# A two-layer graph attention kernel: the residual moves to other buffers, and the list schedule plans with measured transfers

## The chip, the cores and the metric

The kernel runs on one core of a Trainium2 chip. The metric is the device time of one execution in microseconds (us). A run is one execution; where a kernel was run several times the median stands for it.

## The reference, cut to what matters

There are 32 graphs (batches) of 512 nodes with 512 features, each with its own adjacency matrix. Per batch, two graph attention layers follow a layer norm:

```python
h = jnp.maximum(_layernorm(x, axis=-1), 0.0)
x = x + gnn(adj, h, W1, att_src1, att_dst1, b1, W2, att_src2, att_dst2, b2)

def gat_layer(x, mask, W, a_src, a_dst, bias, concat):
    xl = (x @ W).reshape(B, N, H, F)
    asrc = jnp.einsum('bnhf,hf->bnh', xl, a_src)
    adst = jnp.einsum('bnhf,hf->bnh', xl, a_dst)
    e = leaky_relu(asrc[:, :, None, :] + adst[:, None, :, :], 0.2)
    e = jnp.where(mask[..., None], e, -1e9)
    attn = softmax(e, axis=1)
    out = jnp.einsum('bsdh,bshf->bdhf', attn, xl)
    ...
    return out + bias
h = elu(gat_layer(h, mask, W1, ..., concat=True))   # 4 heads of 256
h = gat_layer(h, mask, W2, ..., concat=False)       # 1 head of 512
```

The last line of the computation matters here: the result is the residual x, plus the second layer, plus its bias b2.

## The kernel before, in words

All is float32. Four large products per batch are the work of the tensor engine (PE): the first projection (`project1`, L823), the gathering with the attention weights of layer 1 (`gather1`, L921), the second projection (`project2`, L977), and the gathering of layer 2 (`gather2`, L1055). Apart from the first batch and the last they are done by a scheme of seven half-size products in place of eight (`sevens`, L734): sums of blocks are made beforehand (`sums` L693, `sums1` L874, `sums2` L1029, on the vector engine DVE), and each of the seven partial products is taken from PSUM into its output block by an evacuation: by ACT as a copy where the block is first written, by DVE as an addition or subtraction where it exists.

The attention weights come from class `Soft` (L543): `first` makes the row sums of the softmax (ACT and DVE alternate on tiles named l), `second` makes the weights p (DVE), adds the mask, and takes the exponential (ACT). The mask is added by a transfer that accumulates from DRAM into SBUF (`accumulate`, L324, issued by POOL; rows named `p<-dm`). Vectors are spread over the partitions by a round trip through DRAM (`spread`; rows `das`, `as`, `drr`, `rr`).

The loop over batches is a software pipeline: one turn holds the heads 0 and 1 of layer 1 of batch i+1 (`gather1(s, 0)`), the first projection of batch i+2, the heads 2 and 3 (`gather1(s, 1)`), the gathering of layer 2 of batch i (`gather2`), and the second projection of batch i+1.

Buffers are handed out by `Slots`. Two sets matter here. The four `xr` buffers of 128x512 are the scratch of `elu` (L841: two ACT ops, then one DVE op that writes h1). The four `t` buffers of the same size hold two right-hand sums (t1, t2) for each head of a pair in `sums1`: the first products read them, and the last reader is a subtraction `b21 - t2` (the name `late` in `gather1`), which is queued before the last product of each head.

The residual (`residual`, L1012) takes four `xr` buffers per batch, loads x into them (SP), and lets an accumulating transfer add b2 (POOL). `gather2` adds its products into these tiles (DVE, `put`), and a transfer from there stores the output (SP); then the buffer is free. Batch 30 uses other places for it.

The order of all this is not written by hand. The code only adds jobs to a `Program` (L45) with an engine, a cost in us, what they read and write, and for transfers a size. `order` (L169) makes one order of all 14462 jobs, and each engine's queue follows from it. PE's own order is the order of the code. The others are list schedules: the planner goes backwards from the end (`backwards`), takes each job's latest start as its rank, goes forwards (`forwards`) and, whenever an engine is free, takes the ready job of the best rank (`next_job`). It does so in 12 rounds and keeps the best. A transfer is modelled as one pipe with a lead, a rate and a tail (L53); a wait between two engines costs 0.15 us, and 0.1 us on the same engine (L52).

Of the kernel before, what the change touches and what calls it, by code (L numbers as in the profile page):

```python
# [44 lines left out]
class Program:  # L45
# [5 lines left out]

    CROSS, SAME = 0.15, 0.1  # L52
    DMA_LEAD, DMA_TAIL, DMA_RATE = 1.2, 1.0, 280e3  # L53

# [21 lines left out]
    def latency(self, a, b):  # L76

        if self.jobs[a][0] != self.jobs[b][0]:
            return self.CROSS
        return 0.0 if self.jobs[a][0] == "PE" else self.SAME  # L80

    def forwards(self, rank):

        jobs, after = self.jobs, self.after
        n = len(jobs)
        left = [len(job[2]) for job in jobs]
        ready_at, start, landed = [0.0] * n, [0.0] * n, 0.0
        free, soon, ready = defaultdict(float), defaultdict(list), defaultdict(list)
        tensor = deque(j for j in range(n) if jobs[j][0] == "PE")
        for j in range(n):  # L90
            if not left[j] and jobs[j][0] != "PE":
                heappush(soon[jobs[j][0]], (0.0, j))
        done = []
        while len(done) < n:
            j, t = self.next_job(rank, free, soon, ready, tensor, left, ready_at)
            start[j] = t
            free[jobs[j][0]] = t + jobs[j][1]
            done.append(j)
            if jobs[j][4] is not None:
                landed = max(landed, t + jobs[j][1] + self.DMA_LEAD) + jobs[j][4] / self.DMA_RATE  # L100
            for s in after[j]:
                if jobs[j][4] is not None:
                    r = landed + self.DMA_TAIL
                else:
                    r = t + jobs[j][1] + self.latency(j, s)
                ready_at[s] = max(ready_at[s], r)
                left[s] -= 1
                if not left[s] and jobs[s][0] != "PE":
                    heappush(soon[jobs[s][0]], (ready_at[s], s))
        return start, done  # L110

    def backwards(self, rank):
# [9 lines left out]
        while True:  # L122
            for j in found:
                if jobs[j][4] is not None:
                    moving = max(moving, ready_at[j]) + jobs[j][4] / self.DMA_RATE
                    ready_at[j] = moving + self.DMA_LEAD
                if jobs[j][0] != "PE":
                    heappush(soon[jobs[j][0]], (ready_at[j], j))
# [13 lines left out]

    def next_job(self, rank, free, soon, ready, tensor, left, ready_at):

        best = None
        for e in ("PE", "ACT", "DVE", "POOL", "SP"):
# [4 lines left out]
            elif ready[e]:  # L151
                t = free[e]
            elif soon[e]:
                t = max(free[e], soon[e][0][0])
            else:
                continue
            if best is None or t < best[0]:
                best = (t, e)
# [10 lines left out]
    def order(self):  # L169
# [8 lines left out]
        for j in reversed(range(n)):  # L178
            later = self.DMA_LEAD + self.DMA_TAIL + (jobs[j][4] or 0.0) / self.DMA_RATE
            need[j] = max(  # L180
# [6 lines left out]
            if jobs[j][0] == "PE":  # L187
                if pe is not None:
                    need[j] = max(need[j], need[pe] + jobs[pe][1])
                pe = j  # L190
        rank, best, self.tried = need, None, []
        for _ in range(self.ROUNDS):
            back = self.backwards(rank)
            late = [-back[j] - jobs[j][1] for j in range(n)]
            start, done = self.forwards(late)
            end = max(start[j] + jobs[j][1] for j in range(n))
            self.tried.append(end)
            if best is None or end < best[0]:
                best = end, start, done, late
            rank = [-start[j] - jobs[j][1] for j in range(n)]  # L200
        _, self.start, done, self.late = best
        return done

    def emit(self):
# [5 lines left out]
def tile_gat(  # L210
# [113 lines left out]
    def accumulate(size, reads, writes, to, at, cost=0.95):  # L324
        prog.add(
            "POOL", cost, reads, writes,
            lambda: nc.gpsimd.dma_start(to, at, accum_op=OP.add), 1.4 * size,  # L327
        )
# [25 lines left out]
    def weights1():  # L354
        for c in range(2):
            for r in range(2):
                for k in range(KQ):
                    row = (r * KQ + k) * P
                    ix = AT[r, c]
                    dma(  # L360
                        256e3, (), [("w1", ix, k)], w1_sb[:, ix, k, :, 2:],
                        w1[row : row + P, :].rearrange("p (j c f) -> p c j f", j=H // 2, c=2)[:, c],
                    )

    def scores1():

        vk, bc = ps_.take()
        for a, v in enumerate((as1, ad1)):
            for j in range(H // 2):
                dma(  # L370
                    256e3, (), [vk + ("v", a, j)], bc[:, 2 * a + j, :],
                    bass.AP(tensor=v.tensor, offset=v.offset + j * 2 * FH, ap=[[0, P], [1, 2 * FH]]),
                )
# [20 lines left out]
    def weights2():  # L394

        for (r, c), ix in AT.items():
            dma(
                512e3, [("ht", 0, 0)], [("w2", ix)], w2_sb[:, ix, :, 1 - c : W2H - c],
                w2[r * HF // 2 : (r + 1) * HF // 2, c * DO // 2 : (c + 1) * DO // 2].rearrange(
                    "(k p) f -> p k f", p=P  # L400
                ),
            )
        dma(4e3, (), ["b1"], b1_sb[:, 0], b1.rearrange("(c p) -> p c", p=P))
        dve(TINY, ["b1"], ["b1"], nc.vector.tensor_scalar_mul, b1_sb[:, 1], b1_sb[:, 0], -1.0)
        dma(256e3, (), ["b2"], b2_sb, rows_of(b2, P))
        for a, v in enumerate((as2, ad2)):
            lk, bc = ls.take()
            dma(256e3, (), [lk], bc, rows_of(v[0], P))
            for (r, c), ix in AT.items():
# [24 lines left out]
    def load(b):  # L434
        XT[b] = []
        for t in range(NT):
            xk, xt = xs.take()
            dma(256e3, (), [xk], xt, x[b, t * P : (t + 1) * P, :])
            XT[b].append((xk, xt))

    def masks(b):

        for t in range(NT):
            ak, a = adjs.take()
            dma(256e3, (), [ak], a, adj[b, t * P : (t + 1) * P, :])
            dve(
# [10 lines left out]
        if b < B - 1:  # L457
            MASK[b] = mk, md = mds.take()
            dma(512e3, every, [mk], md.rearrange("p t n -> p (t n)"), m.rearrange("p t n -> p (t n)"))
        tk, mt = mts.take()  # L460
# [4 lines left out]
            ),  # L465
            300e3,
        )
# [22 lines left out]
    def norm_turn(b, t):  # L490
# [3 lines left out]
        act(  # L494
            0.62, [xk, sk + (t,)], [xk], hn, hn, AF.Relu,
            bias=st[:, t, S : S + 1], scale=st[:, t, S + A : S + A + 1],
# [13 lines left out]
        else:  # L510
# [3 lines left out]
            act(  # L514
                1.14, [xk], [ak], words.rearrange("p (h f) -> p h f", h=2),
                hn.bitcast(U16).rearrange("p (f h) -> p h f", h=2), AF.Copy,
# [6 lines left out]
                ),  # L523
                200e3,
            )
            act(
                1.14, [xk], [("ht", t, 0), ("ht", t, 1)],
                ht[:, :, t * P : (t + 1) * P].bitcast(U16).rearrange("p k (n h) -> p h k n", h=2),
# [14 lines left out]
    class Soft:  # L543
# [7 lines left out]
        def spread(self, v, keys, rows, to, through):  # L551
# [11 lines left out]
            dma(  # L563
                0, [ok], [dk], dr[:k].rearrange("k (b j) -> b k j", j=32),
                bass.AP(
# [4 lines left out]
            dma(  # L570
                256e3 * rows, [dk], [ok], o[:, :rows].rearrange("p r n -> p (r n)"),
                bass.AP(tensor=dr.tensor, offset=dr.offset, ap=[[0, P], [1, rows * N]]),
# [67 lines left out]
        def second(self, h):  # L640
# [19 lines left out]
            if not here:  # L660
                mk, md = MASK[self.b]
                for us in (0, 1), (2, 3):
                    keys = p_keys(pk, us)
                    accumulate(
                        500e3, keys + [mk], keys,
                        *(t[:, us[0] : us[-1] + 1].rearrange("p t n -> p (t n)") for t in (p, md)),
# [67 lines left out]
    def sevens(left, right, rkeys, put, kh, units, width, order):  # L734
# [3 lines left out]
        for u, n in order:  # L738
            m = units[u][0]
            acc, first = {1: "a", 2: "g", 5: "b", 6: "a", 7: "a", 3: "b", 4: "a"}[n], n in (1, 2, 5)  # L740
            if first:
# [4 lines left out]
            pe(  # L746
                akeys + rkeys(n), [bk], kh * width / 597,
                [
# [48 lines left out]
    def project1_first(zt):  # L797

        for j in range(H // 2):
            zk, z = zt[j]  # L800
            for t in range(NT):
                for c in range(2):
# [5 lines left out]
                           for q in (("w1", AT[r, c], k), ("w1s", AT[r, c], k, j))],  # L808
                        [bk], KT * 0.435,
                        [  # L810
# [29 lines left out]

    def elu(g, places, at, cost):  # L841

        keys = [("h1", g, r) for r in range(2)]
        ek, e = xrs.take()
        act(cost, [*places, "b1"], [ek], e, at, AF.Exp, bias=b1_sb[:, 0, g : g + 1], scale=-1.0)
        act(0.54, [ek], [ek], e, e, AF.Relu, bias=1.0, scale=-1.0)
# [6 lines left out]
    def gather1_plain(soft, heads):  # L853

        for h in heads:
            pk, p = soft.p.pop(h)
            for f in range(FPH):
                bk, ps = banks.take()
                for s in range(NT):
# [8 lines left out]
                    )  # L868
                elu(h * FPH + f, [bk], ps, 0.6)
                banks.give(bk)  # L870
# [50 lines left out]
    def gather1(soft, j):  # L921
# [4 lines left out]
        for i, n in PAIR:  # L926
# [5 lines left out]
            if first:  # L932
# [4 lines left out]
            pe(  # L937
                akeys + wkeys, [bk], KQ * M / 597,
                [
# [17 lines left out]
            if n in (3, 4):  # L957
                elu(g, [("h1", g, q) for q in range(2)], h1[:, g, :], 0.54)
        for i in range(2):
# [51 lines left out]

    def residual(b, places=(xrs,) * NT):  # L1012

        XR[b] = []
        for d in range(NT):
# [5 lines left out]
            halves = [xk, xk + (0,), xk + (1,)]  # L1021
            dma(256e3, (), halves, xr, x[b, d * P : (d + 1) * P, :])
            if places[0] is xrs:
                accumulate(256e3, [xk], halves, xr, rows_of(b2, P))
            else:
# [29 lines left out]
    def gather2(b, soft, blocks, order=LAST):  # L1055
# [4 lines left out]
        def put(n, u, bk, ps):  # L1060
# [7 lines left out]
            if n == 4 or r == 0 and upper[u[0]] == 0:  # L1068
                upper[u[0]] = -1
                dma(256e3, [xk, xk + (0,), xk + (1,)], (), out[b, d * P : (d + 1) * P, :], xt)  # L1070
                place.give(xk)
# [9 lines left out]
    def gather2_plain(b, soft):  # L1081
# [3 lines left out]
        for d in range(NT):  # L1085
# [8 lines left out]
            dve(0.6, [bk, xk], [xk], nc.vector.tensor_add, xr, ps, xr)  # L1094
            dma(256e3, [xk], (), out[b, d * P : (d + 1) * P, :], xr)
            banks.give(bk)
# [166 lines left out]
```

## Time and profile before

| | us |
|---|---|
| median of 8 runs | 2867.24 |
| lowest and highest | 2855.19, 2873.09 |
| the profiled execution | 2865.74 |
| its span, first to last instruction | 2863.7 |
| busy in the span: DVE | 2584.6 |
| busy in the span: ACT | 2306.0 |
| idle time of ACT ahead of `p<-p,z`, ended by transfers `p<-dm` | 80.0 |
| idle time of ACT ahead of `l<-as,z`, ended by transfers `as<-das` | 97.5 |
| issue to landing of `p<-dm`, median | 5.1 |
| issue to landing of the b2 addition, median | 5.8 |
| mean granted clock of PE, share of full speed | 0.99 |

The engines are PE (matmul), DVE (vector), ACT (scalar), POOL and SP. The work of POOL and SP here is nearly all issuing of transfers. A float32 matmul appears as two records. Nearly every instruction is recorded under the line of a helper (L316 for ACT, L319 for DVE, L322 for SP, L327 for POOL, L333 for PE), so groups are told apart by their tiles: `xr<-mm,xr` is the addition of a product into the residual. A row of the timeline ends with the idle time before it and who ended it. A wait row gives the total in us, the number of times and the longest.

### The profile page before, as it was taken

The page shows a single profiled execution, that of the slowest core. Times are in us where ns is not written, and L with a number is a line of the kernel's source. Part 1 is how long each engine was busy: PE and PEld are TensorE (multiplying, and loading weights), DVE is VectorE, ACT ScalarE, POOL GpSimd, SP SyncE. Part 2 cuts the span into 40 slices and gives each one's busy share as a digit, 9 for nine tenths or more (in the row PEclk, how much of TensorE's full clock was granted, in tenths as well). Part 3 has the DMA queues.
Part 4 walks back from the last instruction along what each step waited for, and adds up shares of the span by engine and source line. Part 5 has one row for each costly group of instructions (what it writes and reads, how often), then busy time and mean ns, then how long its engine had stood idle before and what let it go on. Part 6 is the DMA issues. An engine that isn't in the chain of part 4 may idle for free. (4 is left out here: it accounts for less than half of the span.)

```text
span 2863.7 us, 41534 instructions
## 1 busy us (share of the span) xinstructions
PE 2777.6 (97%) x12456; PEld 2366.0 (83%) x12456; DVE 2584.6 (90%) x6567; ACT 2306.0 (81%) x4861; POOL 418.6 (15%) x466
## 2 busy tenths in 40 slices
PE   7999999999999999999999999999999999999997
PEld 6668887888888888888888888888888888888875
DVE  7969998999989999999899999999998999999995
ACT  6868787888877888887888888888878888888872
POOL 0011111111111111111111111111111111111100
PEclk9999999999999999999999999999999999999999
DMA  6577687777776777877777867778767778778724
GB/s 203 151 162 192 176 215 175 186 196 188 183 196 173 193 196 192 208 187 186 189 186 186 208 174 186 198 192 203 194 173 193 192 184 216 179 185 203 167 67 129
DMA packets 389455, 527.23 MB, mean 184 GB/s; under 512 B 227184, under 2 KB 231280, under 8 KB 389232
## 3 DMA queue, kind: packets, MB, share of 16 engines
q1 hardware_dynamic: 327600, 332.68, 41.5%
q0 software_dynamic: 61632, 191.92, 30.5%
q8 instruction: 99, 1.62, 0.2%
q14 instruction: 124, 1.02, 0.1%
HBM read 344.72 MB, written 50.79 MB: 138 GB/s over the span
## 5 line engine op out<-in xcount | busy, mean ns | idle before, releaser
L333 PE MATMUL mm<-w_sb,hs 128*128 128x257 f32 (+1 forms) x3024 | 694.7, 383 | 20.4 <-ACT xl L316 11.7
L333 PEld LDWEIGHTS mm<-w_sb,hs 128*128 128x128 f32 x3024 | 573.9, 191 | 116.4 <-ACT xl L316 22.7
L327 POOL DMA_DIRECT2D p<-dm x304 | 268.9, 886 | 2038.0 <-DVE p L319 1089.8
L316 ACT ACTIVATE l<-as,z 128x512 f32<-128x512 f32 x640 | 441.8, 724 | 108.7 <-DMA as<-das 97.5
L316 ACT ACTIVATE p<-p,z 128x512 f32<-128x512 f32 x640 | 433.1, 722 | 109.7 <-DMA p<-dm 80.0
L316 ACT ACTIVATE l<-l,low 128x512 f32<-128x512 f32 x640 | 459.3, 723 | 70.7 <-DVE low L319 68.9
L333 PE MATMUL mm<-p,xl 128*128 128x256 f32 (+1 forms) x2016 | 490.2, 391 | 7.3 <-ACT p L316 5.7
L319 DVE SCALAR_TENSOR_TENSOR p<-rr,z 128x512 f32<-128x512 f32 x640 | 456.9, 742 | 40.1 <-DMA rr<-drr 39.6
L333 PE MATMUL mm<-w_sb,ht 128*128 128x258 f32 x2112 | 481.4, 382 | 2.5 <-ACT xl L316 1.5
L333 PE MATMUL mm<-w_sb,h 128*128 128x257 f32 x2056 | 470.0, 380 | 6.0 <-DVE h L319 4.3
L319 DVE CUSTOM_DVE_ANT_1 l<-l,mt 128x512 f32<-128x512 f32 x640 | 426.3, 681 | 43.4 <-ACT l L316 41.8
L333 PEld LDWEIGHTS mm<-w_sb,ht 128*128 128x128 f32 x2112 | 400.5, 190 | 64.3 <-ACT xl L316 3.8
L333 PEld LDWEIGHTS mm<-p,xl 128*128 128x128 f32 x2016 | 382.7, 190 | 84.5 <-issue 18.6
L333 PEld LDWEIGHTS mm<-w_sb,h 128*128 128x128 f32 x2056 | 389.9, 190 | 65.5 <-DVE h L319 5.3
L316 ACT ACTIVATE xl<-mm 128x258 f32<-128x258 f32 (+2 forms) x752 | 282.2, 385 | 55.1 <-PE mm L333 52.6
L319 DVE TENSOR_TENSOR xl<-xl,mm 128x258 f32<-128x258 f32 x558 | 223.7, 416 | 36.4 <-PE mm L333 27.6
L316 ACT ACTIVATE h<-mm 128x256 f32<-128x256 f32 x480 | 175.2, 378 | 78.9 <-PE mm L333 76.7
L316 ACT ACTIVATE xr<-h,b_sb 128x512 f32<-128x512 f32 x240 | 171.4, 723 | 80.9 <-DVE h L319 80.6
L333 PE MATMUL mm<-t,hs 128*128 128x256 f32 x960 | 218.2, 380 | 0.5 <-ACT h L316 0.5
L333 PEld LDWEIGHTS mm<-t,hs 128*128 128x128 f32 x960 | 183.2, 191 | 26.0 <-ACT h L316 0.8
L319 DVE TENSOR_TENSOR xr<-mm,xr 128x256 f32<-128x256 f32 (+1 forms) x424 | 170.1, 415 | 31.3 <-PE mm L333 21.0
L319 DVE SCALAR_TENSOR_TENSOR h<-h,b_sb,xr 128x512 f32<-128x512 f32 x240 | 175.4, 743 | 20.1 <-ACT xr L316 19.5
(105 smaller groups left out, 3423.7 us busy)
## 6 DMA issues: line engine op xcount, KB each, us to landing
p<-dm POOLq DMA_DIRECT2D x304, 512.0 KB, 5.1
rr<-drr SPq DMA_DIRECT2D x160, 512.0 KB
x<-in_x_dram SPq DMA_DIRECT2D x129, 256.0 KB
adj<-in_adj_dram SPq DMA_DIRECT2D x128, 256.0 KB
as<-das SPq DMA_DIRECT2D x64, 512.0 KB
xr<-in_x_dram SPq DMA_DIRECT2D x124, 256.0 KB
xr<-in_L_gnn_b_dram POOLq DMA_DIRECT2D x124, 256.0 KB, 5.8
out_dram<-xr SPq DMA_DIRECT2D x124, 256.0 KB
```

Source lines behind the costliest of these rows:

```text
L316: prog.add("ACT", cost, reads, writes, lambda: nc.scalar.activation(*a, **k))
L319: prog.add("DVE", cost, reads, writes, lambda: f(*a, **k))
L327: lambda: nc.gpsimd.dma_start(to, at, accum_op=OP.add), 1.4 * size,
L333: f(*a, **k)
```

## The change: what it does

Two things. First, the residual takes the four `t` buffers in place of the four `xr` buffers. The loads, the additions of b2, the additions of products and the stores are the same instructions on other tiles. `elu` has the `xr` buffers to itself.

Second, the planner's figures and its search change. Costs of transfers become times in the pipe by kind (0.75 us for 256 KB, 2.2 for a mask addition, 1.56 for a b2 addition, 1.44 for a spread of two rows), lead and tail change, waits between engines differ by pair, and five ACT costs change. SP and POOL are held back while the planned pipe has more than 3.5 us of work ahead of them. After the 12 rounds follow 40 repairs: wherever the planned PE has a gap over 0.05 us, the jobs that lead to it, back to 60 us before, get an earlier rank by twice the gap, and the schedule is made again; the best of all is kept.

```diff
-    CROSS, SAME = 0.15, 0.1
-    DMA_LEAD, DMA_TAIL, DMA_RATE = 1.2, 1.0, 280e3
+    CROSS, SAME = 0.15, 0.07
+    PAIRS = {("PE", "ACT"): 0.21, ("PE", "DVE"): 0.21, ("DVE", "POOL"): 0.58, ("POOL", "DVE"): 0.4}
+    DMA_LEAD, DMA_TAIL, AHEAD = 0.8, 2.0, 3.5
...
-                landed = max(landed, t + jobs[j][1] + self.DMA_LEAD) + jobs[j][4] / self.DMA_RATE
+                landed = max(landed, t + jobs[j][1] + self.DMA_LEAD) + jobs[j][4]
...
+    def sooner(self, rank, start, cause):
+        jobs, lost, free = self.jobs, {}, 0.0
+        for j in range(len(jobs)):
+            if jobs[j][0] != "PE":
+                continue
+            gap, free = start[j] - free, start[j] + jobs[j][1]
+            d = cause[j]
+            while gap > 0.05 and d is not None and start[j] - start[d] < self.SPAN:
+                lost[d] = max(lost.get(d, 0.0), gap)
+                d = cause[d]
+        return [r - self.GAIN * lost.get(j, 0.0) for j, r in enumerate(rank)]
+
+    SPAN, GAIN = 60.0, 2.0
...
+            if e in ("SP", "POOL"):
+                t = max(t, hold)
...
+        for _ in range(self.REPAIRS):
+            rank = self.sooner(rank, start, cause)
+            start, cause = look(rank)
...
+    REPAIRS = 40
...
-            lambda: nc.gpsimd.dma_start(to, at, accum_op=OP.add), 1.4 * size,
+            lambda: nc.gpsimd.dma_start(to, at, accum_op=OP.add), size,
...
-    def residual(b, places=(xrs,) * NT):
+    def residual(b, places=(ts_,) * NT):
...
-            dma(256e3, (), halves, xr, x[b, d * P : (d + 1) * P, :])
-            if places[0] is xrs:
-                accumulate(256e3, [xk], halves, xr, rows_of(b2, P))
+            dma(0.75, (), halves, xr, x[b, d * P : (d + 1) * P, :])
+            if places[0] is ts_:
+                accumulate(1.56, [xk], halves, xr, rows_of(b2, P))
```

## The prediction

> **What bounds the kernel now.** I read the page's first two parts, then who kept the tensor engine waiting, then its timeline and the chain at those waits.
>
> ```profile
> span 2863.7 us, 41534 instructions
> ...
> PE 2777.6 (97%) x12456; PEld 2366.0 (83%) x12456; DVE 2584.6 (90%) x6567; ACT 2306.0 (81%) x4861; POOL 418.6 (15%) x466
> ```
>
> PE is busy 97% of the span. From the timeline a 256-column product takes 1.73 us per eight records (2682.12 to 2683.85), so the 3.24 million columns that the records hold need about 2736 us. That is the floor, and the change touches no product. Only waits and slow clock can be won. The waits of PE are:
>
> ```profile
> PE mm L333 <- DVE hs L319: 19.6, 7, 6.1
> PE mm L333 <- ACT p L316: 14.1, 7, 8.4
> PE mm L333 <- DVE xr L319: 13.9, 18, 2.2
> PE mm L333 <- ACT xl L316: 13.2, 15, 4.4
> PE mm L333 <- ACT x L316: 10.4, 1, 10.4
> PE mm L333 <- DVE h L319: 5.1, 3, 4.3
> ```
>
> With the two rows left out (3.1 and 1.8) it is 81.2 us. By place on the timeline some 30 us lie before 200 us (filling) and 15 us after 2700 us (last batch), where little can be reordered. The rest is spread over the 29 steady batches; its largest pieces are:
>
> ```profile
> 462.57 5.15 PE L333 MATMUL mm<-x,hs 128*128 128x256 f32 x16 [4.14 <-DVE hs L319]
> ...
> 817.82 2.07 PE L333 MATMUL mm<-xl,hs 128*128 128x256 f32 x4 [2.23 <-DVE xr L319]
> ...
> 1687.93 5.16 PE L333 MATMUL mm<-x,hs 128*128 128x256 f32 x16 [3.08 <-DVE hs L319]
> ...
> 2209.52 5.41 PE L333 MATMUL mm<-x,hs 128*128 128x256 f32 x16 [2.72 <-DVE hs L319]
> ```
>
> Each first group should take 3.5 us (16 records) and takes over 5: the clock fell too. The windows around two of them (columns: us, PE, PEld, DVE, ACT, POOL busy, granted clock, DMA share, GB/s):
>
> ```profile
> 810.00:830.00 20.00, 17.23 (x65) 13.96 (x64) 14.73 (x43) 9.53 (x24) 2.59 (x3) 0.83 0.52 127
> ...
> 2205.00:2225.00 20.00, 17.28 (x73) 14.51 (x72) 17.22 (x48) 12.36 (x27) 2.59 (x3) 0.91 0.77 197
> ```
>
> The waits on DVE xr have their reason in the chain (start, length, what):
>
> ```profile
> 2546.34 0.76 DVE h L319
> 2547.12 5.94 DMA xr<-in_x_dram
> 2553.10 0.47 issue
> 2553.58 5.21 DMA xr<-in_L_gnn_b_dram
> 2558.82 0.75 DVE xr L319 x2
> ```
>
> The ELU's last op frees an xr buffer, the residual is loaded into it, b2 is added by a second transfer, and only then can DVE add the product: 12 us in series, started by an op that comes late.
>
> **The change, part by part.** Every engine keeps the same instructions with the same shapes (PE's order is even the same product by product), so no work is removed or added; the planner's further rounds cost nothing on the chip. What moves is order and one set of buffers.
>
> *Residual in the t buffers.* A t buffer is free after the last subtraction that reads t2, which stands before the last two products of each head; an xr buffer only after those products, their evacuations and three ELU ops. In the new queues the fourth b2 add of a batch stands earlier by a median 5.2 us of tensor work (by over 2.5 in 26 of the 31 batches, leaving the first aside), so the 12 us series starts that much sooner. The xr class of waits (13.9 us, longest 2.2) should vanish.
> Moved with it: four loads on SP and four b2 adds on POOL per batch. In the first batch nothing holds them any more, so they go into the filling: four 256 KB loads between batch 1's x loads, and three b2 adds ahead of the small POOL op that finishes batch 1's norm. Cost: at least 0; at most some 4 us, since the third add waits for its load (5.9 us in the chain above) while the norm's own x loads land anyway. The trace spaces its four x loads there by 0.6 us each; two ahead make 1.2 us. I take 1.5.
> The new wait: the first subtraction into a t buffer of the next pair of heads must wait for the store of the residual (116 such pairs of store and op, where the next ELU had waited before, nearly always with 19 us or more of tensor work between). Queued behind it on DVE is everything, evacuations of PSUM included. Between the last add into a buffer and that subtraction the new DVE queue holds 4.7 us of work at the least and 10.4 in the median. The semaphore times of the 124 stores in the trace give 3.6 us from add to landing in the median, under 5.8 in nine of ten, 8.3 at most. [...] By the row about a tenth are late by 1 us or so, some 10 us of DVE, of which PE sees perhaps 3. I take the row, and count it among the new waits below.
>
> *New costs, hold-back and repair rounds.* I weighed them on the queues of the built program. For each product that waited over 0.2 us I added up the step lengths (0.60 us for a 128x512 DVE op, 0.62 and 0.80 on ACT, from the chain) of all that stands on the producer's queue up to the producer, before and after. Measured from the end of the product before, the steady part (200 to 2700 us) has 50 such waits, 45.4 us. For 40 of them, 33.7 us, the producer now stands earlier by more than the wait: every evacuation into the residual (median 2.6 us), and the sums at 1688 and 2209 us by 8.4 and 8.7. Four, 7.4 us, are covered in part, by 4.1; the one at 462 us is of these (2.0 of 4.3, and its exponentials stand 1.0 later, so a transfer may decide it). Six, 4.3 us, are not covered. Recovered: 33.7 + 4.1 = 37.8 us.
> Given back: 22 clusters of products that did not wait have their producer, mostly an ACT evacuation, moved later than its slack, in total 21 us if queue work were time. ACT idles 19% and DVE 10%, so part of it vanishes in idle time: between 0 and 21. But the trace also shows the mask transfers landing after 5.1 us in the median and 6.85 us in the chain at 2594 us, a spread that no order foresees, so I take 15, above the middle.
> *Clock.* [...] after 2.23 us at 817 the window grants 0.83, after 2.72 at 2209 it grants 0.91. [...] by the rows three waits (817, 1688, 2209) bring (0.17 + 0.09 + 0.09) x 20 = 7 us, less what lies in the gaps themselves: 5.5. I take the rows.
> Steady part: -37.8 + 15 - 5.5 = -28.
>
> *Filling and last batch.* Before 200 us three waits are covered (3.4 us), those at 115 and 188 us by 3.2 and 1.2, the sums at 52 us stand 1.5 later, and the residual loads cost 1.5: -5, of which I count -3, as loads decide there. After 2700 us five small waits (2.5) are covered and about as much is moved later; the last 8.4 us wait has no shift: -1.
>
> **Sum.** -28 - 3 - 1 = -32 us on the span: 2832, hence 2834 for the profiled execution (2865.7, which is 2.0 above its span). The median of the runs, 2867.2, is 1.5 above that execution: 2835.
>
> **Rivals.**
> *The given-back waits are as large as the queues allow* (chance 0.15). ACT evacuations are now later in the first product, all 21 us are paid and the clock drops move elsewhere: -37.8 + 21 = -17, nothing at both ends: 2850. For: rows such as ACT xl, 13.2 us, are hardly relieved. Against: the idle shares.
> *It does not carry over* (0.07). The chip's transfers vary as before, and 45 us of waits come back at other places: about 2865. For: the old order had a plan too. Against: the xr class has a structural reason, and that goes.
> *The store holds DVE* (0.05, slower). If stores land later, because loads for the next batch are now queued beside them, each of 29 batches stops DVE at the subtraction. PE has about 1 us of slack there. It turns the sign when the store lands 4.7 + 1 + 1.1 = 6.8 us after its add in every batch (29 x 1.1 = 32); at 7.3 it costs 29 x 1.6 = 46: 2881. Against: nine of ten are under 5.8 today.
> *More comes* (0.08). No new waits at all, 15 us better: 2820.
>
> **How the numbers follow.** Forecast 0.65 (2826 to 2846), rivals 0.15, 0.07, 0.05 and 0.08. A difference under 0.3% (8.6 us) cannot be told from none here, so faster means under 2858.6: the forecast, the better case and most of the first rival, 0.87; same 0.08; slower 0.05. The range takes in the forecast, most of the better case and the first rival with its spread: 2820 to 2857.
>
> **What would show it.** PE's waits fall from 81 to about 50 us; DVE xr nearly disappears from them; DVE hs keeps the 6.1 at the start and part of the 4.1 near 460 us; no clock below 1.00 in the windows near 817, 1688 and 2209; busy times of all engines are as before. POOL's b2 adds come before the last ELU of their batch. Wrong would be: DVE t waiting for stores over 15 us in all, ACT xl waits above 20 us, or a first 200 us longer by over 4 us.

## The result, and the profile after

The changed kernel takes 2848.57 us (median of 11 runs, 2843.21 to 2854.52), the kernel before, run beside it, 2865.98 (32 runs). The ratio is 0.9943, 95% interval 0.9929 to 0.9957: 17 us faster, about half of the 32 forecast. The profiled execution took 2857.45, more than any of those 11 runs, so a second execution of the same program (`same_again` below, 2845.90) is read beside it.

The head of the page, then who kept PE waiting (total us, times, longest), in the first of the two:

```profile
span 2855.7 us, 41575 instructions
...
PE 2770.0 (97%) x12456; PEld 2359.3 (83%) x12456; DVE 2581.6 (90%) x6567; ACT 2310.5 (81%) x4861; POOL 421.1 (15%) x466
```

```profile
PE mm L368 <- ACT p L351: 19.3, 13, 8.6
PE mm L368 <- ACT xl L351: 17.6, 22, 2.5
PE mm L368 <- DVE hs L354: 15.1, 7, 10.5
PE mm L368 <- ACT x L351: 10.2, 2, 9.9
PE mm L368 <- ACT h L351: 7.4, 7, 2.1
PE mm L368 <- DVE t L354: 7.1, 7, 2.9
PE mm L368 <- DVE h L354: 3.0, 4, 1.4
```

With two small rows (1.1 and 0.4) that is 81.2 us, the same sum as before. The residual's row fell from 13.9 (DVE xr) to 7.1 (DVE t, its new buffers) and the sums (DVE hs) from 19.6 to 15.1; ACT's four rows p, xl, x and h rose from 40.8 to 54.5. The span is 8.0 us shorter, and 7.6 of them came from PE's busy time (2777.6 to 2770.0). As no product changed, that is the clock: the time at half clock fell from 55.5 to 41.8 us, worth half of the difference, 6.9 (in the trace before, 16 records of 256 columns took 5.15 us at 462.57, 2.9 of them at half clock, and 3.62 at 1751.91). Five windows of 20 us, of which the second and the fifth were shown before the change (columns as there; the third number from the end is the granted clock):

```profile
420.00:440.00 20.00, 17.50 (x74) 14.70 (x73) 18.13 (x45) 14.75 (x34) 0.30 (x1) 0.91 0.60 156
810.00:830.00 20.00, 20.00 (x94) 17.46 (x93) 19.89 (x48) 13.88 (x31) 3.04 (x4) 1.00 0.65 198
1680.00:1700.00 20.00, 20.00 (x94) 17.44 (x93) 20.00 (x51) 18.21 (x41) 4.45 (x5) 1.00 0.60 176
2157.00:2177.00 20.00, 17.21 (x71) 14.11 (x70) 17.98 (x45) 16.91 (x38) 1.56 (x2) 0.91 0.52 137
2205.00:2225.00 20.00, 19.04 (x87) 16.30 (x88) 20.00 (x56) 17.97 (x42) 4.23 (x5) 1.00 0.48 151
```

The drops near 817, 1688 and 2209 us are gone (0.83 and 0.91 before in the two windows shown then). Two new ones stand near 427 and 2164. They follow new waits, the second and the fourth row here. The first row is the longest wait of all, in the filling; after the third the clock did not fall:

```profile
55.95 0.80 PE L368 MATMUL mm<-w_sb,hs 128*128 128x258 f32 x1 [10.48 <-DVE hs L354]
425.81 0.48 PE L368 MATMUL mm<-w_sb,ht 128*128 128x258 f32 x1 [2.50 <-ACT xl L351]
984.92 0.48 PE L368 MATMUL mm<-x,hs 128*128 128x256 f32 x1 [2.92 <-DVE t L354]
2163.66 0.94 PE L368 MATMUL mm<-w_sb,hs 128*128 128x258 f32 x2 [2.28 <-ACT xl L351]
```

The transfers that POOL issues (KB each, median us from issue to landing) are slower than before, when the masks took 5.1 and the b2 additions 5.8:

```profile
p<-dm POOLq DMA_DIRECT2D x304, 512.0 KB, 5.8
t<-in_L_gnn_b_dram POOLq DMA_DIRECT2D x124, 256.0 KB, 8.5
```

**Old waits and new ones, site by site.** PE does the same products in the same order, so each product can be compared with itself. In the steady part I took the products that waited over 0.2 us for an evacuation or a sum. A wait counts from the end of the product before, which lasts 1.73 us per eight records of 256 columns. The table has the sums in us:

| products | before | after, first execution | after, second |
|---|---|---|---|
| the 40 whose producer now stands early enough | 33.7 | 0.3 | 1.5 |
| the 4 covered in part | 7.3 | 1.8 | 1.8 |
| the 6 not covered | 4.3 | 0.7 | 0.8 |
| products that had not waited | 0 | 46.0 (52 of them) | 35.6 (43) |

So 42.5 and 41.2 us were won, and 46.0 and 35.6 came back elsewhere. 31 of the new sites are the same in both executions (29.4 and 25.8 us there): most of what came back belongs to the order, and about 10 us of it to the execution.

### The profile page after: what moved, and what is told of

It reads as the page before. It is cut to its first block, busy times and chain, and to the rows that moved or that the text cites. A ratio compares the mean times of both kernels' runs of the same rounds, so it can differ in the third digit from the quotient of the medians.

```text
span 2855.7 us, 41575 instructions
## 1 busy us (share of the span) xinstructions
PE 2770.0 (97%) x12456; PEld 2359.3 (83%) x12456; DVE 2581.6 (90%) x6567; ACT 2310.5 (81%) x4861; POOL 421.1 (15%) x466
## 5 line engine op out<-in xcount | busy, mean ns | idle before, releaser
L368 PE MATMUL mm<-w_sb,hs 128*128 128x257 f32 (+1 forms) x3024 | 695.8, 383 | 25.8 <-ACT xl L351 14.6
L368 PEld LDWEIGHTS mm<-w_sb,hs 128*128 128x128 f32 x3024 | 574.4, 191 | 121.9 <-ACT xl L351 25.8
L351 ACT ACTIVATE l<-as,z 128x512 f32<-128x512 f32 x640 | 442.1, 716 | 88.7 <-DMA as<-das 86.1
L368 PE MATMUL mm<-xl,p 128*128 128x256 f32 (+1 forms) x752 | 181.7, 391 | 11.4 <-ACT p L351 10.4
```

What stands on the lines that cost most here:

```text
L351: prog.add("ACT", cost, reads, writes, lambda: nc.scalar.activation(*a, **k))
L368: f(*a, **k)
```

## The experiments

Each ratio is to the kernel before, run on the same chip. A change of the planner or of the buffers gives all queues a new order, so such a run prices that order as a whole; only `b2_narrow` and `store_narrow` keep the order of the changed kernel. First the switches of the change in one table; the runs follow.

| residual in | planner's figures | hold-back | repairs | ratio, 95% interval | run |
|---|---|---|---|---|---|
| xr | old | no | no | 1 | before |
| t | old | no | no | 1.0089 (1.0055 to 1.0124) | res_only |
| xr | old | no | 40 | 1.0018 (1.0006 to 1.0031) | repairs_alone |
| t | old | no | 40 | 0.9907 (0.9883 to 0.9932), again 0.993 (0.991 to 0.995) | old_times, old_times_again |
| xr | measured | yes | 40 | 1.0149 (1.012 to 1.0178) | plan_only |
| t | measured | yes | none | 1.0067 (1.0049 to 1.0084) | no_repair |
| t | measured | no | 40 | 1.0083 (1.006 to 1.0106) | no_hold |
| t | measured | yes | 40 | 0.9943 (0.9929 to 0.9957), again 0.9947 (0.992 to 0.9973) | after, same_again |

**The changed kernel once more (`same_again`).** No edit.

> The changed kernel unchanged, for a second profile beside the others. Its first profiled execution took 2857.5, above all of its 11 runs (median 2848.6), with 81 us of PE waits, as many as before. Theory (order made for mean transfer times; each execution's own transfer times decide which small waits come up): the median is again 2847 to 2851, and the second profile shows PE waits of 70 to 81 us with the small waits in the steady part at partly other places. Rival (the new waits are fixed by the order): the same places wait by the same amounts within 0.3 us.

2852.89 us, ratio 0.9947. Its profiled execution has PE busy for 2767.6 us and waits of 71.9 us, against 2770.0 and 81.2 in the first. Two executions of one program thus differ by some 10 us in PE's waits, and a forecast from one of them can hardly be checked more closely than that.

**The move alone (`res_only`).** The kernel before, its planner untouched, with

```diff
-    def residual(b, places=(xrs,) * NT):
+    def residual(b, places=(ts_,) * NT):
```

> The kernel before with only the residual moved to the t buffers; planner's figures and search as before. Theory (the buffer move alone removes the waits on DVE xr, 14 to 18 us, and gives back few): 2850 to 2855, waits on DVE t under 5 us, the waits on DVE hs at two or more places stay. Rival (without measured times the planner cannot use the freedom): 2862 to 2868, waits on DVE t of 12 us or more.

2890.01 us, slower by 0.9% and outside both expectations. The waits of PE:

```profile
PE mm L333 <- DVE hs L319: 31.4, 24, 3.9
PE mm L333 <- ACT p L316: 28.2, 14, 8.3
PE mm L333 <- ACT xl L316: 13.1, 14, 4.8
```

The waits on the residual did vanish (1.0 us is left), as the prediction had it. But sums and exponentials, 19.6 and 14.1 us before, took more than that back. Freeing a buffer earlier gave the list schedule another order, not a better one.

**The new planner alone (`plan_only`).** The reverse edit on the changed kernel.

> The changed kernel with the residual in the xr buffers as before: new figures, hold-back and repairs alone. Theory (the move is what gains): 2858 to 2866, waits on DVE xr 10 us or more remain. Rival (the schedule gains and the move adds little): 2848 to 2853, waits on DVE xr under 5 us.

2910.78 us, slower by 1.5% and far above both expectations, and the residual is what PE waits for:

```profile
PE mm L368 <- DVE xr L354: 54.7, 44, 4.6
PE mm L368 <- DVE hs L354: 18.5, 16, 3.2
...
p<-dm POOLq DMA_DIRECT2D x304, 512.0 KB, 5.1
xr<-in_L_gnn_b_dram POOLq DMA_DIRECT2D x124, 256.0 KB, 6.0
```

Rows for `xr` went from 13.9 to 54.7 us: in the xr buffers the series of load and b2 addition still begins at the ELU, and the new order leaves it no slack. The masks land as fast as in the kernel before (5.1).

**The changed kernel without repairs (`no_repair`).**

```diff
-    REPAIRS = 40
+    REPAIRS = 0
```

> The changed kernel without the 40 repair rounds (figures, hold-back and move kept). Theory (the repairs close gaps of the plan, which the chip opens elsewhere): within 4 us of the changed kernel, 2845 to 2853. Rival (the repairs carry the gain): 2858 or more.

2886.67 us, slower than before by 0.7%, as the rival had it. Move and measured figures without repairs lose what the whole change wins.

**Narrow b2 additions (`b2_narrow`).** The order of the changed kernel; each addition moves 32 of 512 columns, so the output lacks b2 in the others.

```diff
-                accumulate(1.56, [xk], halves, xr, rows_of(b2, P))
+                accumulate(1.56, [xk], halves, xr[:, :32], rows_of(b2[:32], P))
```

> The changed kernel with every queue in the same order, but each b2 addition of the steady batches moves 32 of 512 columns, so b2 is left out of the other 480. Theory (the waits that took the place of the old ones end in transfers, and the earlier b2 additions lengthen the mask transfers beside them: 5.1 us before, 5.8 after): 6 to 10 us less than the changed kernel beside it (about 2840 to 2846), mask transfers back at 5.1 to 5.3 us, PE waits on ACT p 5 us lower. Rival (the new waits are the order of ACT's and DVE's queues): within 3 us of the changed kernel, 2847 to 2854.

2840.93 us, ratio 0.9894 (0.986 to 0.9928), below the changed kernel's by 0.5%. The interval lies only just below that of the changed kernel's first series (from 0.9929) and overlaps that of its second (from 0.992). The time is where the theory had it, but not by its mechanism, for the masks land no sooner:

```profile
p<-dm POOLq DMA_DIRECT2D x304, 512.0 KB, 5.9
```

So the bytes of b2 may cost something, but they are not why the masks land later. One thing did change: the three longest transposes of the mask (below) land after 11.0 to 12.3 us, where the changed kernel has 17.5 to 19.9. Whether the 0.5% arise there stays open: the profiled execution was the slowest of the four runs.

**Narrow stores (`store_narrow`).** The same order; each store moves 32 of 512 columns, and the rest of the output is not written.

```diff
-   dma(0.75, [xk, xk + (0,), xk + (1,)], (), out[b, d * P : (d + 1) * P, :], xt)
+   dma(0.75, [xk, xk + (0,), xk + (1,)], (), out[b, d * P : (d + 1) * P, :32], xt[:, :32])
```

> The changed kernel with every queue in the same order, but each store out of a t buffer moves 32 of 512 columns, so most of the output of these batches is not written. Theory (a late store stops DVE for some 8 us in all, and PE sees 3): 2844 to 2852. Rival (the wait of the next t buffer for the store is what gives the gain back): 2840 or less, and waits on DVE t and hs fall by 8 us.

2856.79 us, ratio 0.9953 (0.9938 to 0.9967): no gain, as the theory had it. Nor did the edit take the wait away. The first row is the changed kernel, the second this one, whose profiled execution was its slowest run:

```profile
DVE t L354 <- DMA out_dram<-t: 8.3, 3, 4.2
```

```profile
DVE t L354 <- DMA out_dram<-t: 18.8, 6, 5.4
```

The run therefore doesn't price the wait. What does is the first row: three stops of DVE in 116 chances, 8.3 us of an engine that is idle for 274 us of the span.

**Repairs on the old figures (`old_times`, and once more).** The changed kernel, but all planned costs, rates and waits of the kernel before, and no hold-back:

```diff
-    CROSS, SAME = 0.15, 0.07
-    PAIRS = {("PE", "ACT"): 0.21, ("PE", "DVE"): 0.21, ("DVE", "POOL"): 0.58, ("POOL", "DVE"): 0.4}
-    DMA_LEAD, DMA_TAIL, AHEAD = 0.8, 2.0, 3.5
+    CROSS, SAME = 0.15, 0.1
+    PAIRS = {}
+    DMA_LEAD, DMA_TAIL, AHEAD = 1.2, 1.0, 1e9
...
-                accumulate(1.56, [xk], halves, xr, rows_of(b2, P))
+                accumulate(256e3, [xk], halves, xr, rows_of(b2, P))
```

> The move to the t buffers and the 40 repair rounds, but with the figures of the planner before (transfers, waits, ACT costs) and no hold-back. Theory (repairs help only as far as the planned times are those of the chip): 2865 to 2885, with PE waits on masks and spreads. Rival (the repairs alone carry it, whatever the figures): 2843 to 2856.

2847.98 us. My theory at that point was that the repairs gain only because they work on measured times. It fell: without the measured times the kernel shows no loss.

> The same kernel as old_times, once more: residual in the t buffers, 40 repairs, the planner's figures of the kernel before and no hold-back. Theory (the move and the repairs together carry the gain, the measured figures add nothing): 0.990 to 0.995 of the kernel before again. Rival (the first result was a lucky chip): 0.995 to 1.00. The waits of PE should again sum to some 70 to 80 us, at places that differ from those of the first profile where they end in transfers.

2848.81 us. The result holds on another chip. The two intervals overlap with those of the changed kernel, so this version is not shown to be the faster one; it is the smaller change. Measured as in the table of sites, its steady waits are 48.8 and 47.6 us in the two profiles, no fewer than before (45.3). It wins in the filling: the product that began at 204.2 us before begins at 191.9 and 192.4.

**More repairs (`more_repairs`).** `REPAIRS = 160`.

> The changed kernel with 160 repair rounds in place of 40. Theory (what is left of waits comes from transfers that land later than planned, which a better plan does not see): within 5 us of the changed kernel, 2845 to 2855. Rival (the search was cut short): 2842 or less, and steady waits of PE lower by 8 us.

2858.29 us, ratio 0.995 (0.9931 to 0.9969). Four times the search changes nothing that can be measured.

**Repairs alone (`repairs_alone`).** The kernel before with the repairs, everything else old.

> The kernel before with the 40 repairs alone: its own figures, and the residual left in the xr buffers. Theory (move and repairs need each other, as the residual's chain of load and b2 addition starts at the ELU however the queues stand): the waits on DVE xr stay, 14 us or more in all, and the time is 0.997 to 1.003 of the kernel before. Rival (the repairs do it alone, and the move only came with them): 0.990 to 0.995, waits on DVE xr under 5 us.

2875.24 us. The first four wait rows:

```profile
PE mm L368 <- ACT xl L351: 25.3, 35, 2.2
PE mm L368 <- ACT p L351: 11.9, 7, 3.8
PE mm L368 <- DVE hs L354: 11.0, 6, 5.0
PE mm L368 <- DVE xr L354: 10.1, 14, 2.1
```

No gain, and the residual's row stays (10.1 us, I had put 14 or more). Move alone +0.9%, repairs alone +0.2%, both -0.7 to -0.9%: neither half carries the gain, the pair does.

**Without the hold-back (`no_hold`).**

```diff
-            if e in ("SP", "POOL"):
-                t = max(t, hold)
```

> The changed kernel without the hold-back of SP and POOL in the plan; measured figures, move and repairs as they are. Theory A (the hold-back makes transfers late in the plan and so in the queues): 0.990 to 0.993 of the kernel before, like old_times. Theory B (any order of this quality falls within half a per cent, and no single figure decides): 0.993 to 0.998, not to be told from the changed kernel.

2895.03 us, slower than before, where I had allowed no such case: both theories are wrong here. With the measured figures the gain is lost without the hold-back. ACT's idle time ahead of `l<-as,z` that spreads end rose to 128.0 us (82.3 and 86.1 in the two executions of the changed kernel), and PE's waits on the sums to 38.8. The old figures make do without it. They plan 2.5 us in the pipe for a mask where the measured ones have 2.2, 0.91 for a load of 256 KB (0.75) and 1.83 for a spread of two rows (1.44), though 1.28 for a b2 addition (1.56). That the longer figures serve as a margin is my reading; no run tells it apart.

**The first batch's residual kept out of the filling (`first_xr`).**

```diff
-            if places[0] is ts_:
+            if places[0] in (ts_, xrs):
...
-            residual(i)
+            residual(i, (xrs,) * NT if i == 0 else (ts_,) * NT)
```

> The changed kernel, but batch 0 keeps its residual in the xr buffers, so that its four loads and four b2 additions stay out of the filling. If these cost the filling time: the wait of PE on the first sums (DVE hs, 10.5 us in the changed kernel, 6.1 before) falls to 6 to 7 us and the time to 1 to 4 us below the changed kernel, 0.992 to 0.994 of the kernel before. Rival (the order of the sums on DVE does it, not the residual): the wait stays at 9 to 11 us and the time within 3 us of the changed kernel.

2857.18 us, ratio 0.9952 (0.994 to 0.9965): no gain. The wait on the sums did go, and another took its place at once:

```profile
47.01 2.01 PE L368 MATMUL mm<-w_sb,hs 128*128 128x258 f32 x8 [0.44 <-DVE hs L354]
55.15 5.79 PE L368 MATMUL mm<-w_sb,hs 128*128 128x258 f32 x16 [6.13 <-ACT xl L351]
```

The product that began at 55.95 us now begins at 47.01; after its 8 records PE stops for an ACT evacuation, and the next begins at 55.15, 4.4 us ahead of its time in the changed kernel. Three waits on exponentials (2.67, 1.89 and 2.18 us, at 102, 139 and 149 us) use up that lead: the product that began at 198.1 us in the changed kernel and at 196.4 in its second execution begins at 197.2. So an order without the residual's transfers in the filling has its first sums earlier, but its filling ends no sooner.

## Why the forecast held only in part

**What bounds the kernel, and the floor: right.** PE is busy 97% of the span, and DVE and ACT do the same work (2581.6 and 2310.5 us).

**Recovered 37.8 us: right.** 42.5 and 41.2 us. All the covered waits went but 0.3 and 1.5 us; the ten others gave 9.1 and 9.0 where 4.1 were counted.

**The residual class vanishes: half right.** PE still waits 7.1 and 6.7 us for additions into the residual, but none of the steady waits leads back to a b2 addition any more (7.5 us did before, followed as described below). Where an addition is late now, it stands behind other work on DVE's queue: the wait of 2.92 us at 985 us is such a case (below).

**Clock -5.5: right in sum.** PE's busy time fell by 7.6 and 10.0 us. In the steady part the time at half clock fell from 17.1 to 6.8 us in both executions, worth half of the difference, 5.1 us; the rest is at the ends. But the sum has two errors that cancel: the drop at 462 us, which I had kept, went as well (worth 1.7 us), and two new ones came in each execution (worth 3.4 us).

**Filling -3, last batch -1: the filling won more.** The product that began at 204.2 us before begins at 198.1 and 196.4, 6.0 and 7.8 sooner, although the first sums are worse (10.5 and 9.4 us for 6.1): PE's idle time before 200 us fell from 30.0 to 26.6 and 25.3, and the clock did the rest. After 2700 us the idle time stayed (18.9; 19.4 and 19.2).

**The store's 3 us: not measured.** DVE's part, some 10 us in the forecast, is the row of 8.3 us above. What PE sees of it no run shows; none of the steady waits followed below leads to a store.

**Given back 15: this step failed.** It measured 46.0 and 35.6 us. Queue positions, the method of the forecast, found a part: of the new sites 12 and 13 had a producer moved later than its slack, 14.0 and 11.7 us in all. At the other 40 and 30 sites, 32 and 24 us, no producer was moved later than its slack. I had worked on the sentence that every engine keeps the same instructions, and had taken the transfers' durations from the trace of before. But the change starts residual loads and b2 additions earlier, among the masks, spreads and transposes. That late transfers are the cause of those 32 and 24 us is my reading; what the runs show for it and against it follows.

The trace shows that crowding. When a mask addition is issued, 2.0 other transfers were under way on average before, 2.6 in both executions after; `res_only` and `repairs_alone` stand between with 2.3 and 2.2. But the count does not decide the time: `old_times` has 2.7, and `plan_only`, the slowest of all, has 1.9. The first mask of each pair landed after 3.9 us in the median (5.4 in nine of ten) from the end of its issue; now 4.8 (7.4). I followed each steady wait back, from the product to the producer that finished last and along its engine while that ran without a pause, until a transfer or 12 us of work was reached; a pause leads on to whoever ended it. Before, 28.5 of 45.3 us lead to a transfer and 13.7 to a busy ACT or DVE. In the first execution after, 41.1 of 48.8 lead to a transfer (masks 19.6, transposes of the normalized input 7.8, spreads of `as` 7.3, transposes of the mask 5.4, `rr` 1.0) and 5.4 to a busy engine; in the second 28.6 of 39.6, and 8.0. The rest leads to an earlier product. So the share of transfers rose from 63% to 84% and 72%, but in the second execution their sum is what it was before. That is a reading of the semaphores, not an experiment.

One of these chains can be read in full. The timeline of POOL and SP (a transfer's row is its issue) ahead of the wait at 985 us:

```profile
959.28 0.86 POOL L362 DMA_DIRECT2D p<-dm  x1 [11.91 <-DVE p L354]
959.75 0.41 SPq L357 DMA_DIRECT2D t<-in_x_dram  x1
960.82 0.90 POOL L362 DMA_DIRECT2D p<-dm  x1 [0.67 <-PE mm L368]
961.35 3.04 POOL L362 DMA_DIRECT2D t<-in_L_gnn_b_dram  x3
962.67 10.79 SPq L498 DMA_TRANSPOSE mt<-m  x1
...
982.61 0.69 DVE L354 CUSTOM_DVE_ANT_1 l<-l,mt 128x512 f32<-128x512 f32 x1 [3.19 <-DMA mt<-m]
```

Within 5 us a residual load, two masks, three b2 additions and the transpose of the next mask are issued. The transpose takes SP 10.79 us to issue, where the median is 2.9 (1.9 before), and the transfers behind it on SP are issued after that. It lands at 982.6; DVE stood still for 3.19 us, two more `l<-l,mt` follow, and the addition into the residual behind them comes late for PE (the row of 984.92 us above). All issues of this transpose (ns: least, median, most), before and after:

```profile
L463 SPq DMA_TRANSPOSE mt<-m x32: 1560/1918/3857, 32.7 to 2705.1; - x32
```

```profile
L498 SPq DMA_TRANSPOSE mt<-m x32: 1652/2907/13092, 28.6 to 2697.2; - x32
```

Three issues of over 9 us stand at the same three batches in both executions (963, 1656 and 2443 us in the first). At 2443 too it is PE that waits in the end, as the chain shows:

```profile
2443.06 18.41 DMA mt<-m
2461.47 0.02 issue
2461.49 0.69 DVE l L354
...
2466.80 1.14 DVE hs L354
2467.94 0.34 DVE t L354
2468.29 0.04 issue
2468.33 120.83 PE mm L368 x556
```

From issue to landing it took 18.41 us, in the second execution 18.73. These chains hold 5.4 and 3.2 us of the new waits. The long issues do not decide the time: in `first_xr` none takes over 5.0 us and in `old_times` none over 4.5, and the one is as fast as the changed kernel, the other no slower. How much of the masks' delay comes from the residual's transfers and how much from the pairs of masks, which now follow each other after 2.0 us in place of 2.9, stays open. Two runs speak for the former: in `plan_only` and in `old_times` the pairs are 2.5 us apart, and the masks land after 5.1 us with the residual in the xr buffers, after 5.8 with it in t. Two others do not: 5.4 us in `res_only` (t, 2.5 us apart) and 5.5 in `repairs_alone` (xr, 2.8). `b2_narrow` speaks against the bytes of b2 alone. No run moved only the transposes.

**The sum, and the rivals.** In the terms of the profile the forecast was -5.5 us by the clock and -26 by waits. Measured were -7.6 and 0.0 in the first execution, -10.0 and -9.3 in the second; the waits of about 50 us that I had named as the first sign did not come (81.2 and 71.9). By place, the product that began at 204.2 us won 6.0 and 7.8 us against the 3 forecast, and all that follows it won 2.0 and 11.8 against 29. The time came out where the first rival had it (2850), by the mechanism of the second ("the chip's transfers vary as before, and 45 us of waits come back at other places"), which I gave 0.07. I had argued against it that the residual's waits had a structural reason. They had, and these waits went; others came in their place. The median, 2848.6, lies outside the band of the forecast itself (2826 to 2846). It lies within 2820 to 2857 because that range takes in the first rival, not because my sum was right.

## What to carry to other kernels

When one engine is bound at 97%, the waits that a new order removes could be counted from the queues: 37.8 us forecast here, 42.5 and 41.2 measured. What came in their place could not: the queues named 14.0 of 46.0 us, and most of the chains led to transfers. So do not carry the old durations of transfers, or a small allowance for new waits, into a forecast of a new order. Two halves of a change can each be slower and together faster: here the freed buffer gained only in an order that the repairs had fitted to it. Compare two executions of one program first; where they differ by 10 us, a forecast from one of them is no finer than that.

## What the runs showed of the hardware

The clock records of `before` and `after` hold ten and seven stretches at half clock. The last of each ends with the execution (0.92 and 0.80 us); the others lasted 3.41, 6.83, 10.24 or 13.65 us. The length of the gap ahead does not decide it alone: in `after`, the windows grant 0.91 after 2.28 and 2.50 us of idle PE, while after 2.92 us, at 985, the clock stayed at 1.00:

```profile
978.00:998.00 20.00, 17.08 (x79) 14.63 (x78) 16.81 (x48) 12.43 (x31) 0.00 (x0) 1.00 0.51 122
```

So the longest of these three gaps cost no clock. What decides besides the length, these rows do not show.

In `after` the 32 transposes of the mask took SP 1.7 to 13.1 us each to issue. Four of them began while two mask additions issued by POOL had not yet landed, and took 5.27, 9.97, 10.79 and 13.09 us; the other 28 began beside none and took 5.16 us at most. Two such additions did not always go with a long issue: 37 transposes of the adjacency matrix (`x<-adj`) began beside two or more and took 1.3 to 4.2 us. The b2 addition of 256 KB landed after 8.5 us in the median, the mask addition of 512 KB after 5.8.
